# One sandwich layer on one core: less work ahead of the branch, and token norms split over two turns in a fixed order

## The chip, the core and the metric

The kernel runs on one core of a Trainium2 chip. The core has a matrix engine (TensorE, PE in the profile; its weight loads are listed apart as PEld), a vector engine (VectorE, DVE), an activation engine (ScalarE, ACT), a general engine (GpSimd, POOL) and a queue that issues transfers (SyncE, SP). Each engine works through its own list of instructions in order and waits on semaphores for the others. The metric is the device time of one execution in microseconds (us), as a median over runs. Everything is float32 in and out.

## The reference

Input x is 2 batches x 1024 tokens x 512. The layer is an attention block and a feed-forward block, each inside a layer norm and a normed residual:

```
x = x + layernorm(attention(layernorm(x)))
x = x + layernorm(feed_forward(layernorm(x)))
```

The attention has 32 query heads and 8 key and value heads of 128. Its output is the mean of two branches:

```
o_lin: gated linear attention; softmaxed q and k, gate log_sigmoid(k)/16, state 128x128
y:     sliding-window softmax attention with rope, window 64
o = bf16(0.5*y + 0.5*o_lin) @ Wo
```

The feed-forward block quantises its three weights (1376x512, 1376x512, 512x1376) to a 16-value code, 64 values to a block, and back, and then computes `(silu(x w1') * (x w2')) w3'`.

## The kernel before

*A preamble* (lines 1320 to 1363). The fast form of the gated attention is allowed only if the columns of Wk are not too long. So the kernel loads all of Wk into `wka` (four loads of 128 rows), squares it on ACT (`squares`), sums the squares over rows with PE (`norms`), and has DVE take the greatest (`most`) and compare it (`small_gates`, an integer flag). Beside this it loads the first four token chunks (a chunk is 128 tokens) into tiles of their own, `chunks`, norms each (`normed`) and transposes it (`chunk_transposed`: four PE transposes into PSUM, one ACT copy into `xnT`, which holds the normed tokens transposed for all later products). Squares and transposes alternate on PE and ACT. Each engine then reads the flag (line 1364) and branches. With these inputs the fast form is taken.

*A norm* (`norm_stats` and `normed`, lines 152 to 166) is, for one chunk: on DVE `bn_stats`, `bn_aggr` and the adding of epsilon (`ve`), on POOL the power -1/2 (`rstd`, line 161), on DVE again one instruction that subtracts and multiplies (the normalising). The last waits for POOL.

*The turns.* `fast_attention` runs over 128 turns: 8 key heads g, 2 batches b, 8 chunks c (lines 384 and 716). A turn n finishes one chunk for the four query heads of a key head, and prepares the next. On PE it is, in this order: window scores (`ps`), query products of turn n+1 (`pq`), linear attention (`pa`, `ot`), the output projection of turn n-1 (`py`), transposes of rotated and softmaxed queries (`tr`, `tq`), values (`ot` again) and the state product (`pS`). An even turn also computes key and value products for two chunks (`key_products(n + CB)`, tile `pk`), and the odd turn after it makes their gates (`pg`) and transposes (`pt`). ACT copies out of PSUM and takes exponentials, POOL does the rope (`qtmp`, `qr`, `tmp`, `kr`), DVE the masks, maxima, reciprocals and products. From turn 2 on, the quantising of the feed-forward weights (`rounding`, tiles `xw`, `zp`, `zm`, `zs`) is threaded through DVE and ACT as `steps` and `signs`, a fixed number to a turn.

*Order.* `InOrder` wraps an engine. Each instruction given through it is held behind the instruction written before it on that engine. An instruction given to the bare engine (`nc.vector`, `nc.gpsimd`, `nc.scalar`) is put by the scheduler where it thinks best, and a wrapped instruction behind it is held to it alone. In `fast_attention` the names `vector`, `scalar`, `gpsimd` and `tensor` are wrapped, but the norms of token chunks used `nc.vector`, the power used `nc.gpsimd`, and the copies of transposed tokens used `nc.scalar`. All transfers go through bare `nc.sync`.

*Tokens.* Chunks 4 to 15 go through `staging`, eight places in one buffer of the pool that also holds Wo's two float32r parts (`wop`; `part_weights` makes them on POOL with a cast and a subtraction for each head). `inputs` names the chunks of a turn, two in turns 0 and 1, then one, so that chunk 15 comes in turn 9. `input_norms` is called in the middle of a turn, `input_transposes` at its end, which also loads the chunk eight further on. The weights of the next key head are loaded at batch 1, chunk 0, and its `part_weights` is called in batch 1 at chunks 2 to 5.

*The feed-forward's start.* `feed_forward_begun(n)` (line 689), at the end of turns 114 on, loads and transposes quantised weights and, from turn 117, works on the first four chunks of the second block: in one turn `F.tokens` (norm of the attention's output in `yacc`, and the residual), in the next `F.token_norms` (second norm, into `xn`), in the third `F.token_transposes`. After the last turn `F.run` does the rest of the feed-forward block.

*The first turn's preparation* (lines 664 to 677): key products, key softmax and sums, query products, query maximum, gates, decays, query exponentials and softmax, transposes, then two of the four weight parts.

In the profile nearly all instructions that came through a wrapper have line 118, so they are told apart by their tiles.

Of the kernel before, what the change touches and what calls it, by code (L numbers as in the profile page):

```python
# [22 lines left out]
P = 128  # L23
# [98 lines left out]
def sandwich_kernel(ctx: ExitStack, tc: tile.TileContext, x, wq, wk, wv, wo, w1, w2, w3, out, con):  # L122
# [29 lines left out]
    def norm_stats(src, vector):  # L152
# [8 lines left out]
        nc.gpsimd.tensor_tensor(rstd, ve, mhalf, ALU.pow)  # L161
        return mv[:, 0:1], rstd

    def normed(dst, src, vector=nc.vector):
        mean, rstd = norm_stats(src, vector)
        vector.tensor_scalar(dst, src, mean, rstd, ALU.subtract, ALU.mult)
# [110 lines left out]

    def chunk_transposed(xn, ci, ptr, transpose, copy):
# [5 lines left out]
    def fast_attention():  # L284

        with ExitStack() as attn:
# [28 lines left out]

            def input_norms(ci):
                normed(staged(ci), staged(ci))

            def input_transposes(ci):
                chunk_transposed(staged(ci), ci, ptr, transpose, nc.scalar.copy)  # L320
                if ci + 2 * GRP < NCI:
                    chunk_loaded(staged(ci + 2 * GRP), ci + 2 * GRP)
# [340 lines left out]

            key_products(0)
            key_softmax(0)
            key_sums(0)
            query_products(0)
            query_max(0)
# [9 lines left out]

            arriving = iter(range(AHEAD, NCI))
# [9 lines left out]
            def feed_forward_begun(n):  # L689
# [15 lines left out]

                if k >= 2 and k % 2 == 0 and k // 2 - 1 < F.MB:
                    F.token_transposes(k // 2 - 1, early["xn"])
                if k >= 0 and k // 2 < F.MB:
                    if k % 2 == 0:
                        F.tokens(k // 2, early["xc"])  # L710
                    else:
                        early["xn"] = F.token_norms(k // 2)
                if k >= -1 and k % 2 and (k + 1) // 2 < F.MB:
                    early["xc"] = F.load_tokens((k + 1) // 2)

            for n in range(N_):
                g, b, c = chunks[n]
                inputs = list(islice(arriving, 2 if n < 2 else 1))
# [16 lines left out]
                if even:  # L735
# [12 lines left out]
                    for ci in inputs[:1]:  # L748
                        input_norms(ci)
                    if keys2:  # L750
# [14 lines left out]
                    for ci in inputs[1:]:  # L765
                        input_norms(ci)
# [3 lines left out]
                else:  # L770
# [17 lines left out]
                    for ci in inputs[:1]:  # L788
                        input_norms(ci)
                    if more:  # L790
# [10 lines left out]
                    for ci in inputs[1:]:  # L801
                        input_norms(ci)
# [6 lines left out]
                if b == 1 and 2 <= c < 2 + GRP and g + 1 < KVH:  # L809
                    part_weights(g + 1, c - 2)  # L810
# [30 lines left out]
    def general_attention():  # L841

        with ExitStack() as attn:
# [12 lines left out]
            for ci in range(AHEAD, NCI):  # L856
                xc = chunk_loaded(q2p.tile([P, HID], F32, tag="s", name=f"x{ci}"), ci)
# [285 lines left out]
    class FeedForward:  # L1143
# [59 lines left out]
        def tokens(self, ci, xc):  # L1203

            yn = self.next("yn")
            normed(yn, yacc[:, ci, :], self.vector)
# [188 lines left out]
```

## Time and profile before

| | us |
|---|---|
| median of 3 runs | 2147.65 (2146.99 to 2148.22) |
| the profiled execution | 2147.43 |
| its span, first to last instruction | 2145.6 |
| PE busy in the span | 2103.7 |
| DVE busy | 1492.3 |
| ACT busy | 1359.7 |
| POOL busy | 944.6 |
| flag `small_gates` ready | 20.56 |
| first key product behind the branch | 23.92 |
| first scores (turn 0) | 44.83 |
| scores of turn 4 | 108.78 |

Times inside the span count from its start. A timeline line has start, duration, engine, line, operation, result and operands, shape and count; in brackets stands the time that the engine was idle before it, and what it had waited for. PE's records are pipelined: a matmul of 512 columns has two records, which start 0.43 us apart at full clock and 0.86 apart at half.

### The profile page before, as it was taken

To read this page: it belongs to the slowest core of one execution; us is meant where nothing else is said; L and a number is where in the kernel's file an instruction comes from. 1 tells how busy PE (TensorE), PEld (TensorE's weight loads), DVE (VectorE), ACT (ScalarE), POOL (GpSimd) and SP (SyncE) were. 2 spreads that over 40 slices of the span, in tenths; PEclk is the share of its full clock that TensorE was granted. 3 is DMA by queue.
4 is the path that set the end of the run, shared out by engine and by line. 5 is a ranking of instruction groups with operands and counts; after the bars stand their busy time and mean duration, and the time that the engine had idled before them with its cause. 6 is when DMAs were issued, how large, how long until landed. Compare 5 with 4: busy or idle time off the path is not lost.

```text
span 2145.6 us, 27553 instructions
## 1 busy us (share of the span) xinstructions
PE 2103.7 (98%) x8948; PEld 1409.7 (66%) x8948; DVE 1492.3 (70%) x2822; ACT 1359.7 (63%) x3944; POOL 944.6 (44%) x1290
## 2 busy tenths in 40 slices
PE   6899999999999999999999999999999999999998
PEld 3677777777777777777777777777767544444443
DVE  4678888888788888888888888788886342424212
ACT  3688888888888888888888888788875210101000
POOL 4545555655465556546655654565544000000000
PEclk8999999999999999999999999999999999999999
DMA  7000100010010001000100010010100210000000
GB/s 237 20 11 11 60 11 16 25 50 10 11 44 27 14 15 60 11 11 11 58 17 16 22 50 12 11 37 12 35 31 25 61 49 19 20 20 15 20 0 22
DMA packets 45192, 64.52 MB, mean 30 GB/s; under 512 B 3632, under 2 KB 19632, under 8 KB 45040
## 3 DMA queue, kind: packets, MB, share of 16 engines
q1 hardware_dynamic: 45040, 62.67, 9.0%
q8 instruction: 73, 1.20, 0.2%
q14 instruction: 79, 0.65, 0.1%
HBM read 50.01 MB, written 12.65 MB: 29 GB/s over the span
## 4 chain that ended last, share of the span: by engine, by line
PE 87%; ACT 4%; DVE 4%; POOL 3%; issue 1%; DMA 0%; ACTq 0%; POOLq 0%; DVEq 0%
PE pq L118 18%; PE py L118 9%; PE ot L118 9%; PE pk L118 9%; PE pgate L118 7%; PE pout L118 7%; PE pup L118 7%; PE pa L118 7%; PE ps L118 5%; PE tr L118 3%; PE tq L118 2%; PE pg L118 2%; POOL qr L118 2%; ACT ps L118 1%; PE pt L118 1%; PE pS L118 1%
## 5 line engine op out<-in xcount | busy, mean ns | idle before, releaser
L118 PE MATMUL pq<-wq,xnT 128*128 128x512 f32 x1024 | 462.3, 594 | 0.0
L118 POOL TENSOR_TENSOR qtmp<-q,tables 128x512 f32<-128x512 f32 x128 | 162.2, 1268 | 586.8 <-ACT q L118 586.6
L118 PEld LDWEIGHTS pq<-wq,xnT 128*128 128x128 f32 x1024 | 185.6, 191 | 184.7 <-issue 184.7
L118 ACT ACTIVATE zs<-xw,fbounds 128x512 bf16<-128x512 f32 (+3 forms) x416 | 287.9, 723 | 0.0
L118 PE MATMUL py<-wop,oc 128*128 128x512 f32 x1024 | 270.8, 406 | 0.0
L161 POOL TENSOR_TENSOR rstd<-ve,mhalf 128x1 f32<-128x1 f32 x64 | 35.7, 558 | 501.7 <-DVE ve L118 483.8
L118 ACT ACTIVATE ps<-ps,nms 128x128 f32<-128x128 f32 x512 | 175.1, 342 | 117.3 <-DVE nms L118 98.4
L118 ACT ACTIVATE pq<-pq,nmq 128x128 f32<-128x128 f32 x512 | 175.1, 342 | 90.9 <-DVE nmq L118 78.5
L118 PE MATMUL pk<-wkv,xnT 128*128 128x256 f32 x1024 | 232.5, 380 | 0.0
L118 PEld LDWEIGHTS pk<-wkv,xnT 128*128 128x128 f32 x1024 | 195.2, 191 | 47.0 <-issue 15.8
L118 PEld LDWEIGHTS py<-wop,oc 128*128 128x128 f32 x1024 | 183.0, 189 | 35.3 <-issue 0.5
L118 POOL TENSOR_TENSOR qr<-q,tables 128x256 f32<-128x256 f32 x256 | 206.2, 826 | 0.0
L118 DVE SCALAR_TENSOR_TENSOR zp<-zp,zs 128x512 f32<-128x512 f32 (+3 forms) x224 | 195.6, 873 | 8.7 <-ACT zs L118 4.3
L118 POOL TENSOR_TENSOR qr<-qr,qtmp 128x512 f32<-128x512 f32 x128 | 165.3, 1291 | 10.0
L118 DVE SCALAR_TENSOR_TENSOR zm<-zm,zs 128x512 f32<-128x512 f32 (+3 forms) x192 | 164.2, 855 | 5.4 <-ACT zs L118 3.0
L118 DVE TENSOR_TENSOR ps<-ps,fwin 128x512 f32<-128x512 f32 x128 | 89.2, 697 | 101.8 <-PE ps L118 101.2
L118 PE MATMUL ps<-kT,qrT 128*128 128x128 f32 x1024 | 137.4, 278 | 0.2
L118 DVE TENSOR_REDUCE nmq<-pq 128x4 f32<-128x512 f32 x128 | 87.8, 686 | 61.1 <-ACT q L118 61.1
L118 PEld LDWEIGHTS ps<-kT,qrT 128*128 128x128 f32 x1024 | 126.1, 194 | 0.9 <-ACT qrT L118 0.6
L118 ACT ACTIVATE ffqrT<-pgate 128x512 f32<-128x512 f32 (+1 forms) x21 | 12.5, 597 | 176.3 <-PE pgate L118 176.3
L118 PE MATMUL ot<-qh,S 128*128 128x512 f32 x224 | 114.4, 592 | 0.0
L118 ACT ACTIVATE wq<-pgate 128x512 f32<-128x512 f32 (+1 forms) x23 | 13.7, 597 | 153.1 <-PE pgate L118 153.1
(190 smaller groups left out, 4326.6 us busy)
## 6 DMA issues: line engine op xcount, KB each, us to landing
wq<-in_L_attn_Wq_dram SPq DMA_DIRECT2D x8, 1024.0 KB, 5.8
wos<-in_L_attn_Wo_dram SPq DMA_DIRECT2D x8, 1024.0 KB, 5.1
xw<-in_L_ffn_w_dram SPq DMA_DIRECT2D x20, 256.0 KB, 2.6
dq<-zp SPq DMA_DIRECT2D x20, 256.0 KB, 2.0
wos<-dq SPq DMA_DIRECT2D x20, 256.0 KB, 2.6
wq<-_attn_hidden_states_dram SPq DMA_DIRECT2D x16, 256.0 KB, 2.6
out_dram<-ffoc SPq DMA_DIRECT2D x16, 256.0 KB, 2.0
tokens<-_attn_hidden_states_dram SPq DMA_DIRECT2D x12, 256.0 KB, 5.2
```

What stands on the lines that cost most here:

```text
L118: return lambda *args, **kwargs: self.tc.keep_in_program_order(getattr(self.engine, name)(*args, **kwargs))
L161: nc.gpsimd.tensor_tensor(rstd, ve, mhalf, ALU.pow)
```

## The change

The preamble keeps only chunks 0 and 1: they are normed as before, the four squares and their matmuls run without transposes between them, and the two transposes come after. Chunks 0 to 3 are loaded into a buffer that is kept, the place of the second key head's query weights (`first_chunk`: `wqs[1]`), and no longer into tiles of the preamble.

`norm_stats` can now be called by itself, with engines of choice, and `normed` takes its result. In `fast_attention` all norms, powers and copies of tokens go through the wrapped engines. `input_measured(ci)` measures a chunk one turn ahead of its `input_norms`, and each of the turns 0 to 11 handles one chunk. In the preparation of the first turn the query products come first, with the measuring of chunks 2 and 3 ahead of them and their norms and transposes behind; the key products follow. Chunk 4 is measured ahead of the gates.

In the last turns the token work on DVE moves out of `feed_forward_begun` into `feed_forward_tokens`, called in the middle of the turn behind `input_norms`, and there too each measuring comes a turn ahead of its use. Weight parts of the next key head are made at chunks 4 to 7 of batch 1.

```diff
-    def norm_stats(src, vector):
+    def norm_stats(src, vector=nc.vector, gpsimd=nc.gpsimd):
...
-        nc.gpsimd.tensor_tensor(rstd, ve, mhalf, ALU.pow)
+        gpsimd.tensor_tensor(rstd, ve, mhalf, ALU.pow)
...
-    def normed(dst, src, vector=nc.vector):
-        mean, rstd = norm_stats(src, vector)
+    def normed(dst, src, vector=nc.vector, stats=None):
+        mean, rstd = stats or norm_stats(src, vector)
...
+    def first_chunk(ci):
+        return wqs[1][:, ci, :]
...
             def input_norms(ci):
-                normed(staged(ci), staged(ci))
+                normed(tokens_of(ci), tokens_of(ci), vector, input_stats.pop(ci))
+
+            def input_measured(ci):
+                if ci < NCI:
+                    input_stats[ci] = norm_stats(tokens_of(ci), vector, gpsimd)
 
             def input_transposes(ci):
-                chunk_transposed(staged(ci), ci, ptr, transpose, nc.scalar.copy)
-                if ci + 2 * GRP < NCI:
+                chunk_transposed(tokens_of(ci), ci, ptr, transpose, scalar.copy)
+                if AHEAD <= ci < NCI - 2 * GRP:
                     chunk_loaded(staged(ci + 2 * GRP), ci + 2 * GRP)
...
+            for ci in range(2, AHEAD):
+                input_measured(ci)
+            query_products(0)
+            for ci in range(2, AHEAD):
+                input_norms(ci)
+                input_transposes(ci)
+            query_max(0)
             key_products(0)
             key_softmax(0)
             key_sums(0)
-            query_products(0)
-            query_max(0)
+            input_measured(AHEAD)
             key_gates(0)
...
+            def feed_forward_tokens(n):
+                k = n - (L + 5)
+                if k >= 2 and k % 2 == 0 and k // 2 - 1 < F.MB:
+                    early["xn"] = F.token_norms(k // 2 - 1, early["stats"])
                 if k >= 0 and k // 2 < F.MB:
                     if k % 2 == 0:
-                        F.tokens(k // 2, early["xc"])
+                        early["stats"] = norm_stats(yacc[:, k // 2, :], vector, gpsimd)
                     else:
-                        early["xn"] = F.token_norms(k // 2)
+                        F.tokens(k // 2, early["xc"], early["stats"])
+                        early["stats"] = norm_stats(yacc[:, k // 2, :], vector, gpsimd)
...
-                inputs = list(islice(arriving, 2 if n < 2 else 1))
+                inputs = [AHEAD + n] if AHEAD + n < NCI else []
...
-                    for ci in inputs[:1]:
+                    for ci in inputs:
                         input_norms(ci)
+                        input_measured(ci + 1)
+                    feed_forward_tokens(n)
...
-                if b == 1 and 2 <= c < 2 + GRP and g + 1 < KVH:
-                    part_weights(g + 1, c - 2)
+                if b == 1 and NCH - GRP <= c and g + 1 < KVH:
+                    part_weights(g + 1, c - NCH + GRP)
...
-        for ci in range(2):
-            normed(chunks[ci], chunks[ci], vector)
-        squares(0)
-        squares(1)
-        transposed(0)
-        squares(2)
-        transposed(1)
-        squares(3)
-        normed(chunks[2], chunks[2], vector)
+        for ci in range(2):
+            normed(first_chunk(ci), first_chunk(ci), vector)
+        for kt in range(KT):
+            scalar.activation(wka[:, kt, :], wka[:, kt, :], AF.Square)
+            for n in range(2):
+                tensor.matmul(norms[:, n, :], lhsT=ones, rhs=wka[:, kt, n * 512 : (n + 1) * 512], start=kt == 0, stop=kt == KT - 1)
+        for ci in range(2):
+            chunk_transposed(first_chunk(ci), ci, ptr, lambda dst, src: tensor.transpose(dst, src, ident), scalar.copy)
...
         vector.tensor_scalar(small_gates, most1, NORM_MAX, None, ALU.is_le)
-        normed(chunks[3], chunks[3], vector)
-        transposed(2)
-        transposed(3)
```

In an even turn the lines at `input_norms` stand between the query softmax with one of the `steps` and `key_softmax(n + CB)`; in an odd turn they stand behind `collect(n - 1)`.

## The prediction

> **What bounds the kernel now.** The page's first part says which engine carries the span. A busy TensorE (PE) is not an efficient one, but it leaves 2145.6 - 2103.7 = 41.9 us in which it does nothing.
>
> ```profile
> PE 2103.7 (98%) x8948; PEld 1409.7 (66%) x8948; DVE 1492.3 (70%) x2822; ACT 1359.7 (63%) x3944; POOL 944.6 (44%) x1290
> ```
>
> Next, the table by stretches, cut at the first `scores` matmul (tile `ps`) of each turn: 44.83 is turn 0, 64.98 turn 1, and so on. Columns: stretch, its length, then busy time (instructions) of PE, PEld, DVE, ACT, POOL, the granted PE clock, DMA share, GB/s.
>
> ```profile
> 0.00:24.00 24.00, 11.77 (x33) 3.33 (x33) 7.52 (x19) 7.06 (x8) 2.98 (x12) 0.97 0.73 240
> 24.00:44.83 20.83, 12.09 (x42) 7.97 (x41) 9.26 (x27) 7.14 (x23) 15.20 (x26) 0.75 0.85 281
> 44.83:64.98 20.15, 16.79 (x64) 11.94 (x64) 10.78 (x24) 7.84 (x27) 12.25 (x19) 0.79 0.16 55
> 64.98:78.71 13.73, 12.70 (x66) 9.08 (x65) 8.91 (x23) 8.49 (x27) 6.04 (x9) 1.00 0.13 36
> 78.71:96.36 17.65, 15.78 (x71) 11.48 (x69) 11.81 (x29) 10.59 (x32) 9.20 (x13) 0.94 0.09 30
> ...
> 1526.70:1650.11 123.41, 118.65 (x582) 86.52 (x581) 96.31 (x194) 88.53 (x269) 61.38 (x90) 1.00 0.10 31
> ```
>
> Up to 96 us PE is idle for 27 us and runs part of the rest at half clock; from 96 to 1526 it has hardly a gap. So a stall taken out of the first turns shortens the run one for one, and a stall put into a full turn lengthens it one for one. The stretch at 1526-1650 (turns 117 to 125, feed-forward tokens measured) has another 4.8 us idle.
>
> The timeline says what the start waits for.
>
> ```profile
> 20.42 0.14 DVE L118 TENSOR_SCALAR small_gates<-most 1x1 int32<-1x1 f32 x1
> ...
> 23.92 4.66 PE L118 MATMUL pk<-wkv,xnT 128*128 128x256 f32 x16
> ...
> 31.40 0.41 DVE L118 TENSOR_REDUCE nmk<-pk 128x2 f32<-128x256 f32 x1
> ...
> 41.92 1.12 PE L118 MATMUL tr<-ident,qr 128*128 128x128 f32 x4 [3.24 <-POOL qr L118]
> ...
> 44.83 1.91 PE L118 MATMUL ps<-kT,qrT 128*128 128x128 f32 x8
> ```
>
> The flag is ready at 20.56. The keys end at 28.58, but DVE takes their maximum (`nmk`) only at 31.40, being busy with the norms of chunks 4 and 5. POOL ends the query's rope at 41.87, two powers and two weight parts (cast and subtraction) having gone ahead of it.
>
> Last, what a full turn has to spare, from the timelines around turn 8 and turn 119:
>
> ```profile
> 172.04 0.68 DVE L118 TENSOR_TENSOR A<-pa,fcausal 128x512 f32<-128x512 f32 x1
> ...
> 172.77 0.48 PE L118 MATMUL ot<-A,vm 128*128 128x256 f32 x1
> ```
>
> ```profile
> 1555.92 0.55 DVE L118 TENSOR_SCALAR wq<-yacc,mv,rstd 128x512 f32<-128x512 f32 x1 [0.73 <-POOL rstd L161]
> ...
> 1558.65 0.48 PE L118 MATMUL pa<-qh,kT 128*128 128x256 f32 x1 [0.82 <-DVE S L118]
> ```
>
> In turn 8 `A` ends when PE wants it: no slack. In turn 119 PE waits 0.82 us for a DVE that was held by a norm and by that norm's power on POOL.
>
> **The preamble.** The four squares on ACT (1.06 us each) now run as Wk lands instead of waiting for transposes; up to the last quarter 2.6 MB have to land (four of 0.52, two chunks of 0.26), and the table in 2 us steps shows 301 to 407 GB/s from 2 us on: near 9 us, before PE asks for it. PE does the first eight norm records up to 10.71 as now; the other eight follow at the row's spacing of 0.43 us, to 14.15. From there DVE needs 19.00 to 20.56, that is 1.56 us: the flag at 15.75, **4.8 us earlier**. The transposes and copies of chunks 0 and 1 (0.43 and 0.58 us each) lie beside DVE's reduction. The branch itself the trace does not show: between its last transpose load (22.89) and its first load behind the branch (23.89) PE took 1.0 us, with 0.28 of it idle; from the flag to that load it was 3.3. I take 1.0, since PE was at other work for the rest; ends 0.3 and 3.3. First query product at 16.8; Wq (issued 6.32, 9.7 us to land) is there at 16.0. The token loads on SP no longer wait for chunk 3's transposes (24.16 becomes about 17) and land before DVE measures chunk 4.
>
> **From branch to first scores.** Query products 3.44 us, to 20.25; beside them DVE measures chunks 2 and 3 (0.68 + 0.18 + 0.15, about 1.05 us each) and normalises them (0.55 each) after POOL's two powers (0.55), done at about 20.2. Two transposes (0.43 each), key products 3.44: 24.6. `kv` copy 0.6, `nmk` 0.41, gate 0.38 + 0.42, two key exponentials 0.5 each: 27.5. Sums 0.2; then the added measuring of chunk 4, 1.05, in front of the decays: 28.8. Memset 0.3, two `kh` 0.58: 29.8. Transposes at half clock (PE has waited, as now at 37.5) 1.2, `kT` and `eq` copies 0.96, `qrT` 0.6, `tq` partly beside it: scores at **33.0 instead of 44.83: -11.8**. The rope (POOL, 3.9 us from the `q` copy at 20.9) ends at 24.8 and is off the path. Whether pq(0) finds PE at full clock is open: it pauses about 1.4 us, and after the pause 32.02 to 33.42 the clock was still 1.00, after 3.4 us it was 0.62. At half clock it costs 3.4 more.
>
> **Turns 0 to 3.** The floor of a turn is its PE work: 14.22 even (turn 4), 11.85 odd (turn 5), each with one chunk; turn 0, without projection and state, 11.5. Turn 0 stays a chain: scores 1.8 and pq(1) partly at half clock (5.2 as now, at best 3.44; I take 4.6), `q` copy 0.6, `nmq` 0.7, four exponentials 2.0, `qs` 0.9, normalising and measuring 1.5, `nmk` 0.4, gate to `ke` 1.85, `qrT` 0.6: 15.0 against 20.15 (ends: 12.9 with PE at full clock; 18.2 if only the 1.9 us go by which norms held the first mask, 46.74 to 48.66). Turns 1 to 3 get their floors and half a microsecond for what isn't seen: 12.3 against 13.73; 14.8 against 17.65 (DVE's wait of 2.54 us for `rstd` goes, as the power is asked for a turn earlier); 11.9 against 12.42. Together -10.0 (54.0 against 63.95).
>
> **Turns 4 to 11.** Now they carry no norm on DVE, since before's scheduler let the unpinned ones run ahead (all 12 done by 91 us). After, each holds 1.5 us of it in fixed order (0.5 normalising, 1.0 measuring, by start-to-start). Odd turns have it behind `collect`, in 1.7 to 1.9 us of idle: nothing. Even turns have it ahead of `nmk`, on which hang `A` and, through gate and `ke`, the `qrT` copy. Slack by the rows: turn 4, 1.2 plus 0.47 idle: 0; turn 6, 1.18: 0.3; turn 8, 0.05: 1.5; turn 10, 0.74: 0.8. **+2.6** (ends 0 and 12, if all eight pay in full). Two chunks' transposes (0.43 each) move here from turns 0 and 1: +0.9, already taken off there.
>
> **Turns 117 to 125.** Removed: the waits of turns 119 and 121, (0.82 + 0.18 + 0.46) + (0.64 + 0.17 + 0.46) = 2.7. Added ahead of `nmk` in turns 118, 120, 122: 0.5 + 0.6 + 0.95 = 2.05, against slacks of 0.6, 0.7 and 1.35: 1.45 + 1.35 + 0.7 = 3.5. In turn 124 DVE is idle 1.5 before `nmk`: 0. **+0.8** (ends -2.7 and +12).
>
> **What costs nothing.** The weight parts (0.61 + 1.29 us on POOL, 28 times) move two turns later within a half; POOL is 44% busy and they are needed a turn later; were POOL full there, 1.9 us each. Wq of group 1 must wait for chunks 2 and 3 in its buffer (until about 21.4; it now starts at 36.29) and is first read in turn 15. `wos` of group 1 waits for POOL on SP's queue as before; behind it stand only chunks 12 to 15.
>
> Here a rule speaks against the change. The rows: normalising a chunk took 411 / 547 / 1501 ns (min / median / max of 12). The Trainium skill's page "SBUF — State Buffer", section "Summary: rules for kernel authors", says that a VectorE instruction in its two-port mode and a GpSimd instruction block each other until the first has finished. By that rule each normalising pinned beside a rope step costs 0.95 more, in the six even turns without slack 5.7, and the sum would be 2136.
>
> **Sum.** -11.8 - 10.0 + 2.6 + 0.9 + 0.8 = -17.5: span 2128.1. The profiled execution took 2147.43, that is 1.8 around its span, and lies 0.2 below the median of 2147.65: **2130**.
>
> **Rivals.** (1) *Further down:* turn 0 near its floor and no stall behind: -17.5 - 2.1 - 2.6 - 3.5 = -25.7, 2122. Against it: turn 8's row above. (2) *A slow start:* half clock for pq(0) (3.4), a branch of 2.5 (1.5 more) and turn 0 at 18 (3): -17.5 + 7.9 = -9.6, 2138. For it: clocks of 0.75 and 0.79 in the two stretches. (3) *The branch moves and little else:* only the 4.8 reaches the first scores, because another wait replaces POOL's: -17.5 + 7.0 = -10.5, 2137. Against it: DVE's and POOL's delays are named norms and casts. (4) *Slower:* DVE's fixed order. Each of the 16 turns 4 to 11 and 117 to 124 loses its added work in full, with normalising at its slowest (1.50): 12 turns x 2.45 + 4 x 3.0 = 41.4 against a gain of 23.6 before any such stall (17.5 + 2.6 + 3.5): +17.8, 2165. It decides from a mean stall of 1.5 us in these turns. For it: DVE is 80% busy; against it: the idle 1.7 to 1.9 us in odd turns.
>
> **Chances.** The forecast 0.60, with 2124 to 2136 as its own range; (1) 0.12; (2) and (3) together 0.17; (4), mostly in part, 0.11. The range 2121 to 2143 holds the first three cases, and leaves out most of the last and the tails of the others. No change is within 0.2% (4.3 us), about what a measurement can tell: faster 0.88, same 0.06, slower 0.06.
>
> **What would show it.** Right: `small_gates` near 15.8, first `ps` near 33, second near 48, `ps` of turn 4 near 87; no `tokens` row of DVE ahead of `nmk` in the first turn; waits of PE `ot` on `A` of 1 to 1.5 us in turn 8 and in turns 118 and 120; none on `S` in 119 and 121. Wrong: `ps` later than 38; PE idle over 10 us between 100 and 210; clock below 1.00 during the first `pq`.

## The result and the profile after

The changed kernel takes **2135.35 us** (median of 4 runs, 2134.87 to 2135.92). The kernel before, run beside it, takes 2147.93 us (4 runs, 2146.99 to 2148.49). The ratio is 0.9942, with a 95% interval of 0.9925 to 0.9959. So the change saves 12.6 us, where 17.5 were forecast (2130 us). The profiled execution took 2135.78 us, with a span of 2133.7 against 2145.6.

The first part of the page of the changed kernel gives each engine's busy time:

```profile
PE 2100.2 (98%) x8948; PEld 1406.2 (66%) x8948; DVE 1495.1 (70%) x2822; ACT 1358.1 (64%) x3944; POOL 947.1 (44%) x1290
```

PE does the same 8948 recorded matmuls. Its idle time is 33.5 us (2133.7 less 2100.2) instead of 41.9, and its busy time fell by 3.5, with less of the work at half clock. The table by stretches of the changed kernel shows where; it is cut at the flag and then at the first scores of turns 0, 1, 2, 3, 4, 12, 117 and 126. Columns as in the prediction (length, busy time of PE, PEld, DVE, ACT and POOL, PE clock, DMA share, GB/s).

```profile
16.67:33.55 16.88, 11.70 (x48) 8.16 (x49) 6.93 (x20) 7.54 (x25) 10.82 (x21) 0.92 1.00 317
33.55:47.41 13.86, 12.61 (x60) 9.37 (x59) 7.08 (x15) 7.30 (x26) 9.39 (x13) 0.97 0.20 73
...
75.11:88.65 13.54, 12.29 (x62) 8.52 (x60) 12.17 (x26) 11.30 (x34) 6.17 (x10) 1.00 0.05 19
88.65:198.38 109.73, 106.24 (x509) 77.37 (x510) 93.64 (x183) 83.87 (x249) 58.17 (x81) 1.00 0.04 13
1513.76:1638.26 124.50, 119.11 (x583) 87.14 (x581) 97.07 (x194) 88.37 (x269) 61.66 (x90) 1.00 0.10 30
```

The clock column is 0.92 and 0.97 where it was 0.75 and 0.79, and turn 0 has 1.25 us without PE work instead of 3.36. But turns 4 to 11, the line at 88.65, now have 3.49 us without PE work (109.73 less 106.24); the kernel before had 0.09 there:

```profile
108.78:211.72 102.94, 102.85 (x502) 76.20 (x501) 83.64 (x154) 85.15 (x249) 54.65 (x75) 1.00 0.04 11
```

Laid side by side, each row from the first scores of its first turn:

| stretch | before, us | after, us | difference | forecast |
|---|---|---|---|---|
| start to first scores | 44.83 | 33.55 | -11.28 | -11.8 |
| turns 0 to 3 | 63.95 | 55.10 | -8.85 | -10.0 |
| turns 4 to 11 | 102.94 | 109.73 | **+6.79** | **+3.5** |
| turns 12 to 116 | 1314.98 | 1315.38 | +0.40 | 0 |
| turns 117 to 125 | 123.41 | 124.50 | +1.09 | +0.8 |
| turn 126 to the end | 495.49 | 495.44 | -0.05 | 0 |
| sum | 2145.60 | 2133.70 | -11.90 | -17.5 |

By turn 4 the changed kernel was 20.1 us ahead. One third of that was given back in the next eight turns.

The start itself went nearly as planned, as the timeline of the changed kernel shows (start, duration, engine, operation; in brackets the idle time before it and what ended it; wrapped instructions have line 117 in this kernel):

```profile
16.53 0.14 DVE L117 TENSOR_SCALAR small_gates<-most 1x1 int32<-1x1 f32 x1
...
17.67 3.67 PE L117 MATMUL pq<-wq,xnT 128*128 128x512 f32 x8 [1.57 <-ACT xnT L117]
22.05 3.62 PE L117 MATMUL pk<-wkv,xnT 128*128 128x256 f32 x16
26.32 0.42 DVE L117 TENSOR_REDUCE nmk<-pk 128x2 f32<-128x256 f32 x1 [3.58 <-ACT kv L117]
33.55 1.47 PE L117 MATMUL ps<-kT,qrT 128*128 128x128 f32 x8
```

The key maximum `nmk` now follows the keys at once, because no norm of chunks 4 and 5 stands before it. From the flag (16.67) to the first query product (17.67) is 1.0 us, so the branch costs no more than that, and the products run at their full-clock length of 3.67 us after a pause of 1.57 us.

**The unexpected loss, in odd turns.** This is the end of turn 3 in the changed kernel, from the timelines of DVE, POOL and PE:

```profile
85.56 0.54 DVE L117 TENSOR_SCALAR tokens<-tokens,mv,rstd 128x512 f32<-128x512 f32 x1
...
86.95 0.15 DVE L117 TENSOR_SCALAR ve<-mv 128x1 f32<-128x1 f32 x1
87.18 0.93 POOL L117 TENSOR_TENSOR rstd<-ve,mhalf 128x1 f32<-128x1 f32 x1 [1.94 <-DVE ve L117]
88.06 0.54 POOL L117 COPY kT<-kT 128x64 f32<-128x64 f32 x1
88.54 0.28 POOL L117 COPY khz<-kT 128x128 f32<-128x128 f32 x1
88.65 1.16 PE L117 MATMUL ps<-kT,qrT 128*128 128x128 f32 x8 [0.74 <-POOL kT L117]
```

POOL's rope of the queries ended at 85.24, and ACT's `kT` copy at 85.80. POOL could then have copied its piece of `kT`. But in its queue the power `rstd` of the next chunk comes first, and that waits 1.94 us for DVE, which normalises this chunk and measures the next one before it has `ve` ready. The key copies follow the power, and the scores of turn 4 wait for them. In the kernel before no power stood there; in turn 5, for example, the copy waited for ACT alone:

```profile
133.08 0.29 POOL L118 COPY khz<-kT 128x128 f32<-128x128 f32 x1 [0.65 <-ACT kT L118]
```

The longest waits of PE over turns 2 to 11 of the changed kernel (in total, times, longest):

```profile
PE ps L117 <- POOL kT L117: 2.5, 4, 0.7
PE ot L117 <- DVE A L117: 1.4, 2, 1.2
PE tr L117 <- POOL qr L117: 0.8, 2, 0.5
```

The first row is the new wait, four times, in the odd turns 3, 5, 7 and 9. The second is the forecast one, in even turns (2 and 8 here). The third, for POOL's rope of the queries in turns 3 and 5, is new as well; e1_pool comes back to it. Turn 8 shows the full form of the forecast wait in the timelines of DVE and PE:

```profile
154.31 0.54 DVE L117 TENSOR_SCALAR tokens<-tokens,mv,rstd 128x512 f32<-128x512 f32 x1
...
156.10 0.68 DVE L117 TENSOR_TENSOR A<-pa,fcausal 128x512 f32<-128x512 f32 x1
...
156.84 0.70 PE L117 MATMUL ot<-A,vm 128*128 128x256 f32 x2 [1.20 <-DVE A L117]
```

The norms of chunk 12 and the measuring of chunk 13 lie between 154.31 and 155.85, ahead of `nmk` and `A`, and PE waits 1.20 us for `A`. The same wait stands in turns 118, 120 and 122 (0.89, 1.49 and 0.61 us), with feed-forward tokens in place of chunks; the timeline of PE has that of turn 120 as

```profile
1568.36 0.70 PE L117 MATMUL ot<-A,vm 128*128 128x256 f32 x2 [1.49 <-DVE A L117]
```

### The profile page after: what moved, and what is told of

Read it like the earlier page. It is cut to its first block, busy times and chain, and to the rows that moved or that the text cites. A ratio compares the mean times of both kernels' runs of the same rounds, so it can differ in the third digit from the quotient of the medians.

```text
span 2133.7 us, 27561 instructions
## 1 busy us (share of the span) xinstructions
PE 2100.2 (98%) x8948; PEld 1406.2 (66%) x8948; DVE 1495.1 (70%) x2822; ACT 1358.1 (64%) x3944; POOL 947.1 (44%) x1290
## 4 chain that ended last, share of the span: by engine, by line
PE 86%; DVE 5%; ACT 5%; POOL 2%; issue 1%; DMA 0%; ACTq 0%; POOLq 0%; DVEq 0%
PE pq L117 17%; PE py L117 9%; PE pk L117 8%; PE ot L117 8%; PE pgate L117 7%; PE pout L117 7%; PE pup L117 7%; PE pa L117 6%; PE ps L117 5%; PE tr L117 2%; PE tq L117 2%; ACT ps L117 2%; PE pg L117 2%; ACT pq L117 1%; POOL qr L117 1%; PE ptr L117 1%
## 5 line engine op out<-in xcount | busy, mean ns | idle before, releaser
L160 POOL TENSOR_TENSOR rstd<-ve,mhalf 128x1 f32<-128x1 f32 x42 | 23.0, 548 | 466.0 <-DVE ve L117 466.0
```

## The experiments

The first three kernels ask what the given-back 6.8 us is, the fourth what the preamble is worth, and the others which of the remaining parts carries the gain. Theory A: in odd turns POOL's power, waiting for DVE, holds the key copies; in even turns DVE's norms hold `A`; each wait goes when the norm's calls stand behind the work that they hold up. Its rivals: the cost is DVE's load as such, or the added transposes (two chunks of 0.43 us, so 0.86 of the 6.8). All diffs are against the changed kernel unless said otherwise.

Spans are those of one execution each. Eight of the kernels (the changed one, e1 to e3 and e5 to e8) have the same preamble, and their flags still lie between 16.09 and 17.00, so up to 0.9 us in a difference of spans can be scatter of the start (see the last section). Where it matters, the difference of the medians stands beside that of the spans.

### Odd turns: norms behind the key copies (e1_pool)

```diff
                     collect(n - 1)
-                    for ci in inputs:
-                        input_norms(ci)
-                        input_measured(ci + 1)
-                    feed_forward_tokens(n)
                     if more:
                         key_transposes(n + 1)
                         rope_transposes(n + 1)
...
+                    for ci in inputs:
+                        input_norms(ci)
+                        input_measured(ci + 1)
+                    feed_forward_tokens(n)
                     values(n)
```

> Against the changed kernel, in odd turns the normalising, measuring and feed-forward token block stands behind the key and rope transposes, so the power on POOL queues behind POOL's copies of the keys (kT, khz, eq) instead of ahead of them; DVE's order is the same. Theory A (the power held the copies that the next scores need): the waits of scores on POOL kT (0.74, 0.74, 0.32, 0.65 us, ahead of turns 4, 6, 8, 10) go, turns 3, 5, 7 and 9 come to within 0.3 us of 11.85, and the span falls by 2.5 to 4 us from 2133.7. Rival B (odd turns are late because DVE's queue is full, POOL only shows it): the wait moves to the score masks or qrT and the span falls by less than 1 us.

Measured: 2131.37 us (2130.92 to 2131.61), ratio to before 0.9923 (0.9906 to 0.9939), span 2129.3, which is 4.4 below the changed kernel (4.0 between the medians). Of the 4.4, 0.45 lies ahead of the first scores, where the two kernels are alike. The end of turn 3 in this kernel, from POOL's and PE's timelines:

```profile
84.25 0.23 POOL L117 COPY kT<-kT 128x64 f32<-128x64 f32 x1
84.92 0.38 POOL L117 COPY khz<-kT 128x128 f32<-128x128 f32 x1 [0.43 <-ACT kT L117]
...
86.24 0.92 POOL L117 TENSOR_TENSOR rstd<-ve,mhalf 128x1 f32<-128x1 f32 x1 [0.90 <-DVE ve L117]
...
86.82 1.06 PE L117 MATMUL ps<-kT,qrT 128*128 128x128 f32 x8
```

The copies now end before the power begins, and the scores no longer wait. Turn 3 falls from 13.54 to 12.66 us, turn 5 from 13.27 to 12.38, turn 7 from 12.52 to 12.02, turn 9 from 12.82 to 12.02. Together that is 3.1 us, and as DVE does the same norms in the same turns, its cause is POOL's queue.

It isn't the whole loss of the odd turns. Turns 7 and 9 came within 0.3 us of 11.85, as expected; turns 3 and 5 did not, and turns 5 to 11 (odd ones, without the moved transposes) are still 1.2 us longer than in the kernel before. PE's waits over turns 2 to 11 of this kernel have one that remains:

```profile
PE tr L117 <- POOL qr L117: 0.9, 2, 0.5
```

The rows point at DVE's load here. DVE comes late out of an even turn, so the first mask of the odd turn is late, and behind it the exponentials, ACT's `q` copy and POOL's rope of the queries. In turn 5 the mask began 1.09 us after the first scores in the kernel before (123.00), and begins 1.79 us after them in the changed kernel (102.97) and in e1_pool alike; the two lines are from the kernel before and from the changed one:

```profile
124.09 0.70 DVE L118 TENSOR_TENSOR ps<-ps,fwin 128x512 f32<-128x512 f32 x1 [0.38 <-PE ps L118]
...
104.76 0.69 DVE L117 TENSOR_TENSOR ps<-ps,fwin 128x512 f32<-128x512 f32 x1
```

No run separates this part. The wait of `ot` on `A` in even turns stays (from turn 0 on four times, 2.7 us).

### Even turns: norms behind the masked products (e2_dve)

```diff
                     query_softmax(n + 1)
                     steps(1, n)
+                    if keys2:
+                        key_softmax(n + CB)
+                    mix(n)
                     for ci in inputs:
                         input_norms(ci)
                         input_measured(ci + 1)
                     feed_forward_tokens(n)
-                    if keys2:
-                        key_softmax(n + CB)
-                    mix(n)
```

> Against the changed kernel, in even turns the same block stands behind the mixing product A instead of ahead of the key maximum nmk. Theory A (1.5 to 2.05 us of DVE work ahead of nmk and A hold the values product and the qrT copy): the waits of ot on A in turns 2, 8, 118, 120 and 122 and of qrT in turn 2 go, the even turns 2, 6, 8, 10, 118, 120, 122 lose 0.5 to 2 us each and the span falls by 5 to 8 us from 2133.7. Rival B (DVE is full in an even turn and only hands the delay on): turns get shorter by what the next ones get longer, the span falls by less than 2 us.

Measured: 2128.17 us (2127.92 to 2128.38), ratio 0.9908 (0.9891 to 0.9924), span 2126.3, 7.4 below the changed kernel (7.2 between the medians). DVE's timeline in turn 8 of this kernel has the order turned round:

```profile
150.60 0.41 DVE L117 TENSOR_REDUCE nmk<-pk 128x2 f32<-128x256 f32 x1
150.94 0.67 DVE L117 TENSOR_TENSOR A<-pa,fcausal 128x512 f32<-128x512 f32 x1
151.53 0.97 DVE L117 TENSOR_SCALAR tokens<-tokens,mv,rstd 128x512 f32<-128x512 f32 x1
```

Turn 8 falls from 15.23 to 14.02, turn 2 from 15.67 to 14.32, turn 118 from 15.76 to 14.31, turn 120 from 15.41 to 13.35. A part comes back one turn later: turns 9, 119 and 121 are about 1 us longer (13.90, 14.28 and 14.31 against 12.82, 13.34 and 13.21). The power is still ahead of the key copies in odd turns: the wait of the scores on `kT` remains (four times, 2.6 us). The edit also puts POOL's power behind the key rope in even turns; that the wait was DVE's is read from the rows (`A` waits for nothing on POOL).

### Both (e3_both)

The two diffs above together, against the changed kernel:

```diff
 even turns:
+                    if keys2:
+                        key_softmax(n + CB)
+                    mix(n)
                     for ci in inputs:
...
 odd turns:
                         rope_transposes(n + 1)
...
+                    for ci in inputs:
...
                     values(n)
```

> Both moves at once. Theory A: the two stalls are on different queues and add up: the span falls by 8 to 11 us from 2133.7, median near 2126. Rival B: less than 3 us.

Measured: **2124.41 us** (2124.1 to 2125.37), ratio 0.989 (0.9874 to 0.9907), span 2123.6, 10.1 below the changed kernel. The two effects add up to within 2 us (4.4 and 7.4; some 0.5 of each of the three is the earlier start). The waits of PE in this kernel over the same turns as above are down to

```profile
PE tr L117 <- POOL qr L117: 0.8, 3, 0.5
PE pa L117 <- DVE sw L117: 0.2, 1, 0.2
```

Turns 4 to 11 take 105.74 us instead of 109.73; the kernel before took 102.94, or 103.8 with the two moved chunks' transposes. This kernel beats both the one before (by 23.6 us) and the changed one (by 10.9).

### The preamble of before in the changed kernel (e4_preamble)

```diff
-        for ci in range(2):
-            normed(first_chunk(ci), first_chunk(ci), vector)
-        for kt in range(KT):
+
+        def squares(kt):
             scalar.activation(wka[:, kt, :], wka[:, kt, :], AF.Square)
...
-        for ci in range(2):
+
+        def transposed(ci):
...
+        for ci in range(2):
+            normed(first_chunk(ci), first_chunk(ci), vector)
+        squares(0)
+        squares(1)
+        transposed(0)
+        squares(2)
+        transposed(1)
+        squares(3)
+        normed(first_chunk(2), first_chunk(2), vector)
...
+        normed(first_chunk(3), first_chunk(3), vector)
+        transposed(2)
+        transposed(3)
```

The calls that measure, normalise and transpose chunks 2 and 3 behind the branch go.

> The changed kernel with the preamble of before: squares and transposes alternate and chunks 2 and 3 are normed and transposed ahead of the branch, not behind it. Theory A (the flag's time reaches the end of the run one for one, as the first turn is a chain): flag back at 20.6, first query product near 24 instead of 17.67, two chunks' work less behind it, first scores 5 to 6 us later than 33.55, span 5 to 6 us longer, median near 2141. Rival C (the branch moves and another wait takes its place): first scores less than 2 us later.

Measured: 2143.31 us (2142.32 to 2143.91), ratio 0.9978 (0.9968 to 0.9987), span 2140.6, 6.9 above the changed kernel (8.0 between the medians), more than the 5 to 6 expected. PE's timeline of this kernel:

```profile
24.81 5.19 PE L117 MATMUL pq<-wq,xnT 128*128 128x512 f32 x8 [0.23 <-SPq L1408]
...
41.34 1.15 PE L117 MATMUL ps<-kT,qrT 128*128 128x128 f32 x8
```

The first query product starts 7.14 us later than in the changed kernel, and takes 5.19 us instead of 3.67: PE had waited 3.37 us for chunk 3's norm before the last transposes, and the clock fell. The first scores come at 41.34 instead of 33.55. The turns behind it are as in the changed kernel (13.53 / 12.01 / 15.67 / 13.54). The flag was expected at 20.6 and came at 21.59, because PE's slow pace at the start lasted longer than in the kernel before (the last section; the transposes behind the first eight records begin at 11.73 against 10.71); some 1 us of the difference is therefore scatter. So the preamble is worth some 6 to 8 us, and the rest of the change some 5 (2145.6 less 2140.6; 4.7 between the medians).

### Keys ahead of queries in the first turn (e5_keys_first)

```diff
-            query_products(0)
+            key_products(0)
             for ci in range(2, AHEAD):
                 input_norms(ci)
                 input_transposes(ci)
-            query_max(0)
-            key_products(0)
             key_softmax(0)
             key_sums(0)
+            query_products(0)
+            query_max(0)
             input_measured(AHEAD)
```

> The changed kernel with one thing put back: behind the branch the key products and key softmax of the first turn stand ahead of the query products, as in the kernel before; chunks 2 and 3 stay behind the branch. Theory (what held the first scores was work of norms and weight casts on the queues, not the order of queries and keys): key products end near 21.3, query products near 25, POOL's query rope 3.9 us after the query's copy at about 25.6, so near 29.7; first scores between 32 and 34.5 (33.55 in the changed kernel), span -1.5 to +1 us against 2133.7. Rival (query products first is itself a main part of the gain, because POOL's rope of the queries then runs beside the keys): first scores at 36.5 or later, span +3 us or more.

Measured: 2135.43 us (2134.34 to 2135.75), ratio 0.994 (0.9923 to 0.9956), span 2133.5, 0.2 below the changed kernel. First scores at 32.65 instead of 33.55; turn 0 gives half of that back. The waits change their place, as PE's list up to 34 us shows:

```profile
PE pt L117 <- DVE kh L117: 2.4, 1, 2.4
...
PE tr L117 <- POOL qr L117: 1.2, 1, 1.2
```

The order of queries and keys is worth nothing here.

### Norms of chunks 4 to 15 free again (e6_free)

```diff
             def input_norms(ci):
-                normed(tokens_of(ci), tokens_of(ci), vector, input_stats.pop(ci))
+                if ci >= AHEAD:
+                    normed(tokens_of(ci), tokens_of(ci))
+                else:
+                    normed(tokens_of(ci), tokens_of(ci), vector, input_stats.pop(ci))
 
             def input_measured(ci):
-                if ci < NCI:
+                if ci < AHEAD:
```

> The changed kernel with the norms of chunks 4 to 15 taken out of the written order again (measured and normalised as one, placed by the scheduler as in the kernel before); the feed-forward tokens, the preamble and the first turn's order stay. Theory (the pinned norms cost about 6.8 us in turns 4 to 11 and save in turns 0 to 3): the norms run ahead as soon as their chunks are loaded, so the first scores or turns 0 to 3 become 5 to 9 us longer, and turns 4 to 11 take 6 to 7 us less; span +4 to -2 us against 2133.7. Rival 1 (the pinning carries most of the gain in the first turns): turns 0 to 3 longer by 12 us or more, span +6 or more. Rival 2 (pinning only costs): turns 0 to 3 as in the changed kernel within 1 us, span -5 or lower.

Measured: 2136.67 us (2136.1 to 2137.19), ratio 0.9948 (0.9931 to 0.9964), span 2134.0, 0.3 above the changed kernel (1.3 between the medians). The expectation holds in kind: first scores at 37.81 (4.3 later) and turns 0 to 3 together 56.66 us (1.6 longer), together 5.8 where 5 to 9 were expected; then turns 4 to 11 104.51 us, 5.2 shorter where 6 to 7 were expected. DVE's timeline of this kernel has the reason for the later start:

```profile
31.46 1.17 DVE L165 TENSOR_SCALAR tokens<-tokens,mv,rstd 128x512 f32<-128x512 f32 x2 [0.81 <-POOL rstd L160]
...
34.65 0.58 DVE L117 SCALAR_TENSOR_TENSOR kh<-ke,rsk,pg 128x128 f32<-128x128 f32 x2
```

Four chunks are normalised or measured ahead of `kh`, which stands at 34.65 instead of 30.18. Fixing the order of the norms moved their cost from the start to turns 4 to 11; by itself it gained nothing.

### Measured and normalised in the same turn (e7_same_turn)

```diff
                     for ci in inputs:
+                        input_measured(ci)
                         input_norms(ci)
-                        input_measured(ci + 1)
```

(in both places; `input_measured(AHEAD)` ahead of the turns goes)

> The changed kernel without the lead of one turn for chunks 4 to 15: each chunk is measured and normalised in the same turn, at the same place of the written order; nothing else is changed. Theory (measuring ahead only hides POOL's power from DVE): DVE waits about 0.9 us for the power between measuring and normalising in each of turns 0 to 11; turns 0 and 2 and the even turns from 6 on, where PE waits for DVE already, become 0.5 to 1 us longer each, while in the odd turns the power is asked for 0.5 us earlier and the wait of the scores on the key copies shrinks a little; span +2 to +6 us against 2133.7. Rival 1 (the lead is worth nothing, since PE's wait is for the power and not for DVE): within 1 us. Rival 2 (it is most of the first turns' gain): turns 0 to 3 longer by over 5 us.

Measured: 2144.6 us (2143.86 to 2146.21), ratio 0.9986 (0.9976 to 0.9996), span 2143.0, 9.3 above the changed kernel, more than expected. DVE in turn 0 of this kernel:

```profile
43.56 0.15 DVE L117 TENSOR_SCALAR ve<-mv 128x1 f32<-128x1 f32 x1
44.37 0.94 DVE L117 TENSOR_SCALAR tokens<-tokens,mv,rstd 128x512 f32<-128x512 f32 x1 [0.66 <-POOL rstd L117]
```

DVE waits 0.66 us for the power (0.9 expected). By the rows, two things had been left out. The normalising now falls beside POOL's key rope in even turns (0.94 or 0.95 us) and beside its key copies in odd ones (0.62 or 0.70), so it takes 619 / 818 / 947 ns (min / median / max of 12) instead of 534 / 538 / 807. And it comes so late in odd turns that the chunk's transposes wait for it too, as PE's waits from 90 us on show:

```profile
PE ot L117 <- DVE A L117: 5.3, 4, 2.3
PE xtp L117 <- DVE tokens L117: 2.7, 4, 0.7
```

Turns 0 to 3 are 4.9 us longer, just short of the 5 that rival 2 asked for, and turns 4 to 11 another 4.8. So with a fixed order the lead of one turn is worth 9.3 us. Without a fixed order (e6_free) little is lost by leaving it out, since the scheduler runs the norms ahead by itself.

### Two chunks in each of the first two turns (e8_two_chunks)

Against e6_free:

```diff
-                inputs = [AHEAD + n] if AHEAD + n < NCI else []
+                inputs = [ci for ci in ([AHEAD + 2 * n, AHEAD + 2 * n + 1] if n < 2 else [AHEAD + n + 2]) if ci < NCI]
...
-                    for ci in inputs:
+                    for ci in inputs[:1]:
                         input_norms(ci)
...
                     steps(2, n)
+                    for ci in inputs[1:]:
+                        input_norms(ci)
```

(the last two hunks in even and in odd turns)

> The changed kernel with the norms of chunks 4 to 15 out of the written order (as in the variant with free norms, span 2134.0, first scores at 37.81, turns 0 to 3 together 56.7 us, turns 4 to 11 104.5), and now also with two chunks in each of the turns 0 and 1 and one in each of the turns 2 to 9, as in the kernel before. Theory (in the kernel before part of the long turns 0 to 3 was the second chunk of the turn, whose norms, transposes and copies stand ahead of the masks and the next turn's transposes): turns 0 to 3 together 3 to 6 us longer than with one chunk, turns 4 to 11 shorter by the 0.9 of two chunks' transposes and copies or somewhat more, span +2 to +5 against 2134.0. Rival (one chunk or two makes no difference, the same work is moved): turns 0 to 3 at most 1.5 us longer and turns 4 to 11 as much shorter, span within 1 us.

Measured: 2142.35 us (2141.55 to 2143.42), ratio 0.9975 (0.9966 to 0.9985), span 2141.4, 7.4 above e6_free (5.7 between the medians, as this profiled execution is the slowest of its ten runs). Turns 0 to 3 take 59.54 us, 2.9 longer, and turns 4 to 11 102.95, 1.6 shorter, near what was expected. But the first scores also moved, from 37.81 to 43.31, and that wasn't expected. POOL's and DVE's timelines of this kernel:

```profile
28.00 0.61 POOL L117 CAST wop<-wos 128x512 fp32r<-128x512 f32 x1 [1.18 <-DMA wos<-in_L_attn_Wo_dram]
...
32.93 0.72 POOL L117 TENSOR_TENSOR tmp<-kv,tables 128x256 f32<-128x256 f32 x1
...
36.38 1.17 POOL L160 TENSOR_TENSOR rstd<-ve,mhalf 128x1 f32<-128x1 f32 x2
36.97 1.16 DVE L165 TENSOR_SCALAR tokens<-tokens,mv,rstd 128x512 f32<-128x512 f32 x2 [5.66 <-POOL rstd L160]
```

With another list of chunks the scheduler put two weight parts (cast and subtraction, and 1.18 us of waiting for Wo) ahead of the key rope, although the kernel writes them behind it. In the kernel before they had come ahead of the query's rope in the same way. The key rope starts at 32.93 instead of 27.43 in e6_free, the power behind it at 36.38 instead of 30.88, the scores at 43.31 instead of 37.81: 5.5 us each time, of which 0.7 was there already at the first query product (18.00 against 17.31). In the changed kernel the first of them starts at 32.44, behind all that the first scores need. So part of what the change won at the start is this order on POOL. A likely reason, which no run tests: in this kernel and in the one before, turn 0's second norm, whose power is free, is written directly ahead of turn 0's two weight parts, so these are held to that power alone; with one chunk to a turn an ordered instruction stands there.

### The squares alone, in the kernel before (e9_squares_first)

Against the kernel before:

```diff
-        squares(0)
-        squares(1)
-        transposed(0)
-        squares(2)
-        transposed(1)
-        squares(3)
+        for kt in range(KT):
+            squares(kt)
+        transposed(0)
+        transposed(1)
```

> The kernel before with one part of the change alone: ACT squares the four quarters of Wk back to back, and the transposes of chunks 0 and 1 follow them; chunks 2 and 3 are still normalised and transposed ahead of the branch, and everything behind the branch is as before. Theory (only the place of the branch moves): the flag near 16.7 instead of 20.56, the first key product near 20 instead of 23.92 because chunk 3's norm and the two transposes follow the flag, first scores 3 to 4 us earlier than 44.83, later turns unchanged, span 2141.5 to 2143 against 2145.6. Rival (behind the branch the norms and weight casts set the end whatever the flag does): first scores within 1 us of 44.83, span within 1 us of 2145.6. Further rival (the earlier token loads collide with the weights): first scores later than 45.

Measured: 2143.47 us (2142.78 to 2144.53), ratio 0.9981 (0.9971 to 0.999), span 2141.5, 4.1 below the kernel before (4.5 between the medians). DVE and PE of this kernel:

```profile
17.07 0.14 DVE L118 TENSOR_SCALAR small_gates<-most 1x1 int32<-1x1 f32 x1
...
20.43 3.69 PE L118 MATMUL pk<-wkv,xnT 128*128 128x256 f32 x16 [0.23 <-issue]
```

The flag is 3.4 us earlier, the first scores are 3.5 earlier (41.31), and turns 1 to 13 and 116 to 126 are as long as before to 0.15 us. An earlier branch reaches the end at least one for one even while the norms behind it stay in the way.

## Why the prediction was right, and where it was wrong

The sign, the range and the mechanism of the start held; the mechanism in the odd turns did not. The size was 5.6 us too large on the span, and 3.3 of that is one term. The measured 2135.35 us lies near the upper end of the forecast's own range (2124 to 2136), and the figures of two rivals, 2137 and 2138, are nearer to it than 2130, though neither of their mechanisms came.

**The preamble (4.8 forecast, 3.9 measured).** The flag came at 16.67, not 15.75. The branch was taken at 1.0 and is 1.0. The missed 0.9 us is the row for the first norm matmuls: six of them ran at 0.85 us each before the spacing dropped to 0.43, where in the kernel before it had been four (see the last section). The row gave one execution's length of that slow start, and was taken as fixed.

**From the start to the first scores (-11.8 forecast, -11.28 measured).** Right, and for the reasons given: no norm holds up `nmk`, no weight part stands ahead of the query's rope, and the two powers that do are over at 20.47, before the query's copy. From the flag on, it took 16.88 us (17.25 forecast). What was open, the first query product at full clock, came out as taken (3.67 us). The other case is seen in e4_preamble, where a pause of 3.37 us made it 5.19.

**Turns 0 to 3 (-10.0 forecast, -8.85 measured).** Turn 0 took 13.86 (15.0 forecast), because its second query product ran at full clock, 3.60 us rather than the 4.6 taken; turn 1 took 12.03 (12.3). Turns 2 and 3 took 15.67 and 13.54 (14.8 and 11.9): they already hold the waits of the next term, which the forecast counted only from turn 4 on. Turn 3 was also taken without the half microsecond that the sum says it gives to turns 1 to 3: 11.85 and 0.5 would be 12.35, not 11.9.

**Turns 4 to 11 (+3.5 forecast, +6.79 measured): the step that failed.** It is the sentence "Odd turns have it behind `collect`, in 1.7 to 1.9 us of idle: nothing". The even turns were sized right: turns 4, 6, 8 and 10 grew by 0.10, 0.57, 1.31 and 1.00, together 2.98, which is 2.55 without one moved chunk's transposes (0.43), against the forecast 2.6. The odd turns 5, 7, 9 and 11 grew by 1.42, 0.80, 0.98 and 0.61, together 3.81, or 3.4 without the other chunk's transposes, against 0. The idle time was looked up on DVE alone, and in a kernel whose even turns carried no norms yet. But the norm's power is on POOL, and that it had become pinned there was in the diff (`gpsimd` passed to `norm_stats`). Behind it on POOL stand `kT`, `khz` and `eq`, on which the next scores wait. e1_pool shows it: with the same DVE work and the power behind those copies, the wait is gone and turns 5, 7 and 9 are 2.2 us shorter (turn 3 another 0.9). The other 1.2 us stay in e1_pool; by the rows they are DVE work of the even turn running over into the odd one, and that part is read, not tested.

**Turns 117 to 125 (+0.8 forecast, +1.09 measured).** Right in kind: the waits on `S` in turns 119 and 121 went (-1.92 and -1.94), and waits on `A` came in turns 118, 120 and 122 (+1.39, +2.05, +1.18; forecast 1.45, 1.35 and 0.7). Both sides are about 1 us larger than forecast (-3.9 against -2.7, +4.6 against +3.5), so that the net figure came out near because two errors cancelled.

**What costs nothing.** The moved weight parts, loads and Wo were taken at 0 between turn 12 and turn 116, and that stretch grew by 0.40 us in 1315; among the variants that leave it as it is, it lies between 1314.77 and 1315.51 too. No run undid this part alone.

**The rule on blocking.** The Trainium skill's page "SBUF — State Buffer", section "Summary: rules for kernel authors", would have added 0.95 for each of six normalisings. In the changed kernel the rows are 534 / 538 / 807 ns: in turns 2 to 10 POOL's query rope had ended before the normalising began (153.40 against 154.31 in turn 8), and there was nothing to block. Where the two overlap, in turn 0 (0.81 us) and in the even turns of e7_same_turn (0.94), it is 0.27 and 0.40 us longer, not 0.95; of POOL's instruction 0.52 (42.68 to 43.20) and 0.65 us (44.37 to 45.02) were left to run. That the rule's total of 2136 lies so near the measured time is luck. The other direction did matter: in turn 3, beside DVE's `zp` operations, POOL's power took 0.93 us instead of 0.55 and its `kT` copy 0.54 instead of 0.24, and the scores wait for both. That agrees with the page in kind (it names a VectorE instruction with two inputs in that memory as the other case that blocks), though no run separated it.

**The rivals.** *Further down* asked for no stall in turns 4 to 11; its opposite came, though e3_both, with the stalls removed, goes to 2124.4, 2.4 us from that rival's 2122. *A slow start* would have given -9.6, and none of its three terms came: the first query product took 3.67 us, the branch 1.0, turn 0 13.86. *The branch moves and little else* would have given -10.5; the amount is near, but the way isn't: 20.1 us were gained by turn 4. *Slower* was to decide from a mean stall of 1.5 us in 16 turns. The stalls put in there, without the moved transposes and before the removed waits on `S`, are 10.5 us (5.93 in turns 4 to 11, 4.62 in turns 118, 120 and 122), 0.66 a turn.

**Which part carries the gain.** Of the 11.9 us of span, some 6 to 8 are the preamble (e4_preamble); of these some 4 are the order of squares alone (e9_squares_first, from the other end). In the remaining 5, one chunk instead of two in turns 0 and 1 is worth 5.7 to 7.4 with free norms (e8_two_chunks), 4.8 of it by a later key rope on POOL. The written order of the norms is nearly neutral (e6_free, 0.3 to 1.3), and the measuring a turn ahead is what makes it so (e7_same_turn, 9.3). These numbers don't add up to the whole, because the parts remove some of the same waits.

## What to carry to other kernels

When an operation with a part on a second engine is given a fixed place, look at both queues at that place: here DVE had 1.7 us to spare, and POOL's 0.55 us power still cost 3.1 us in four turns, because it waited for DVE with the next turn's key copies behind it. A place is free only if what stands behind each piece, on each engine, is not wanted before the piece's own input is ready; moving the calls by a few lines, behind the copies and behind the product that PE wants next, gave 10.9 us, nearly as much again as the whole change. Shortening the chain ahead of a branch paid at least one for one (e9_squares_first), and sparing PE a pause of 3.37 us there paid twice, since the products behind it then kept their full clock (3.67 us against the 5.19 of e4_preamble). A single profiled execution is no fixed price for the start: with the same preamble the flag came between 16.09 and 17.00.

## What the runs showed of the hardware

The norm matmuls at the start don't have one speed. The weight loads of PE in the changed kernel mark the start of each:

```profile
9.84 0.13 PEld L117 LDWEIGHTS norms<-wka,ones 128*1 128x1 f32 x1 [0.72 <-issue]
10.62 0.09 PEld L117 LDWEIGHTS norms<-wka,ones 128*1 128x1 f32 x1 [0.65 <-issue]
11.05 0.08 PEld L117 LDWEIGHTS norms<-wka,ones 128*1 128x1 f32 x1 [0.34 <-ACT wka L117]
```

Up to 10.6 they come every 0.8 to 0.85 us, from then on every 0.43. In the kernel before the same change of pace came at 8.9, although PE began at the same 5.6:

```profile
8.11 0.13 PEld L118 LDWEIGHTS norms<-wka,ones 128*1 128x1 f32 x1 [0.73 <-issue]
8.90 0.09 PEld L118 LDWEIGHTS norms<-wka,ones 128*1 128x1 f32 x1 [0.66 <-issue]
```

In e3_both it came at 9.2, in e1_pool at 9.7 and in e6_free near 10, with the same preamble as the changed kernel; in e4_preamble and e9_squares_first the pace was still the slow one at 10.75. So the slow start lasted from 3.3 us to over 5 us from PE's first work, and 0.9 us of the flag's place is that. The table by stretches shows a clock of 1.00 (third column from the end) there all the same:

```profile
0.00:16.67 16.67, 10.47 (x24) 2.37 (x24) 4.55 (x11) 6.48 (x7) 1.88 (x10) 1.00 0.94 317
```

Here the spacing of the records tells more than that column does. The Trainium skill's page "TensorE: Matmul & The Clock Gate", section "Part 1: The HAM clock gate (the "warmup" mystery)", says that the array starts at half rate for about 3.4 us of time, with a window that runs freely, so that the length varies from run to run. The runs agree that the length varies, and the longest cases here were at least half as long again as the page's figure.

After a pause the cases seen in the first query products are 1.57 us, with the products at full pace (3.67 us for eight), and 3.37 us, with 5.19 us for the same eight. In e9_squares_first a pause of 2.04 us ahead of the last transposes left the key products at full pace (3.69 us, where the kernel before took 4.66 after 3.38). Which length between these slows the next products down was not separated.
